# A residual turned by way of DRAM and VectorE instead of TensorE, with five smaller edits, in a two-layer hybrid kernel on one core

## The chip, the core and the metric

The kernel runs on one core of a Trainium2 chip. The core has five engines, each with its own queue of instructions, worked off in order: TensorE (PE; PEld is its weight load), VectorE (DVE), ScalarE (ACT), GpSimd (POOL) and SyncE (SP), which only issues DMAs. Engines wait for each other through semaphores. The metric is the device time of one execution in microseconds (us).

## What is computed

All in float32. Layer 0 (group norm, windowed attention, small linear layers) makes tokens `t` of shape 2 x 4096 x 128. Layer 1, which the change touches, is

```
t = t + attn(ln(t))        # full attention of 4096 tokens, 2 images
t = t + ffn(ln(t))         # STU: long convolution by FFT + three lags
```

with, cut to what matters,

```
def _L1_attn_ref(q):
    sim = einsum('blh,bmh->blm', q, q) * scale      # diagonal masked
    return einsum('blm,bmh->blh', softmax(sim), q)

def _stu(u, ...):
    return _compute_spectral(u, ...) + _compute_ar_u(Mu, u)   # spectral part + lags 0, 1, 2
```

The second line's `t` is the *residual*: the result of the attention layer, which has to be added to the ffn's result at the end. Attention leaves it with tokens on the partitions; the output needs channels on the partitions, so it has to be turned.

## The kernel before

Layer 0 fills the first 348 us and runs into the start of attention. Then, for image b = 0 and b = 1, `attention(b, fill)` walks over 36 pairs of chunks of 512 tokens. For a pair it makes scores on PE (L926, L935), exponentials on ACT (L931, L942), and two sums on PE (`other`, L1057, and `own`, L984). For most pairs the exponentials are turned by a DMA to DRAM and back (`eb`, `et`, L965) and DVE's 32 x 32 transposes (L974). The near pair (6, 7), one of the last, is turned on PE instead: `turned_here` (L976) makes four transposes of 128 x 128 on PE and one copy on DVE (L981), once at each of the pair's four steps, and the `own` product of a part comes one step after it.

After each step `fill()` lets other work run one piece further: `after(b, c)` (L1117) finishes chunk c: it divides, adds the residual in place into `tt[b]` (tokens on partitions), normalizes, turns the result and makes the forward transform; `room()` and `fresh()` (L1100, L1106) send the transform `us` to DRAM through POOL's queue, two places or so behind. `filters()` (L1338) makes the transforms of the filters into DRAM (`gs`); their negatives are written into two places in turn (L1393, L1394), each read by a store.

`short_lags(b, h)` (L1202) has two parts for each half h of an image. The first (four pieces) turns the residual: 4 x 4 PE transposes of `tt[b]` and an ACT copy of 128 x 512 into `xa[b]` (L1210). The second (four pieces) makes the lags: three matmuls of 128 x 512 in PE (L1220), and DVE adds the result, scaled, onto `xa[b]` (L1236, four or eight instructions). `residual_of` (L1399) puts the first part in the queue of fill pieces. After `attention(1)` the last chains, the remaining lags and the last residual pieces are run out (L1545 to L1561).

The ffn's main loop works in 160 *blocks*: `burst` (L1589) multiplies the loaded `ct` (filters) and `ut` (input) into four PSUM banks `pc`, which DVE and ACT copy to `y` (L1603), two banks each, and calls the loads of the block four or five further on: one `ut` and four `ct` DMAs on SP. A group of four blocks is projected (`project`, L1617, into the four banks `acc`) while the next group's bursts are put in between, one before each eight k. `mixed_bins` (L1623) combines a group: copies of `acc` on DVE and ACT (`af`), the rest on POOL. When an image's 16 groups of a chunk are there, `back` (L1648) transforms them back in eight places (par, f): PE transposes of `ob` (L1669), ACT copy `t` (L1670), and at the next step four matmuls (L1656), added by DVE onto `xa[b]` (L1662). A step is put in after k = 4 and k = 12. `finished` (L1709) and, for the last image, the tail (from L1771) add `xa` and send the output.

In the main loop only PE's order is the program's (`manual_schedule(engines={PE})`). The order on DVE, ACT, POOL and SP is laid down when the kernel is built, by a planner with its own costs. All queues are in order on the chip.

Of the kernel before, what the change touches and what calls it, by code (L numbers as in the profile page):

```python
# [14 lines left out]
P = 128  # L15
NB = 2
# [86 lines left out]
def kernel(  # L103
# [769 lines left out]

    us = dram.tile([NB, 2, Q, 2, 2, SG, FB, P], F32, name="us")
    gs = dram.tile([Q, 2, 2, SG, GROW], F32, name="gs")

    with ap_:
        tp = ap_.enter_context(tc.tile_pool(name="l1_t", bufs=1, side="right"))
# [22 lines left out]
        def attention(b, fill):  # L901
# [135 lines left out]
            for i, (a, c) in enumerate(pairs):  # L1037
# [6 lines left out]
                for j in range(4):  # L1044
                    if tt[1] is not None and not ordered:
                        ordered.append(written.enter_context(tc.manual_schedule(engines={engines.PE, engines.DVE, engines.Activation, engines.Pool, engines.SP})))
                    due = late and late[0][0] <= step
                    while following and len(coming) < min(4, j + (2 if j == 0 and a != c and not due else 1)):
                        coming.append(coming_of(*following, len(coming), coming, halves))
                    n = 4 * CHUNKS[a] + j  # L1050
                    turn = lambda v, o: v.rearrange(o, q=4, t=4) if far(a, c) else v
                    if j == 0:
                        pass_on(2)
                    if a == c:
                        onto(owns[a], n, owns[a], es[j], j == 0, a == 7 and j == 3)
                    else:
                        nc.tensor.matmul(  # L1057
                            turn(other, "p (q t j) -> p q t j"), lhsT=tok[b][:, n, :], rhs=es[j],
                            start=(j == 0), stop=(j == 3),
                        )  # L1060
                    if a != c and j == 3:
                        xs, ov = xa[b][:, chunk(c)], other
                        if far(a, c):
                            xs, ov = xs.rearrange("p (t q j) -> p q t j", t=4, q=4), ov.rearrange("p (q t j) -> p q t j", q=4, t=4)
                        if a:
                            nc.vector.tensor_tensor(xs, ov, xs, ALU.add)  # L1066
                        else:
# [49 lines left out]
        def after(b, c):  # L1117
# [84 lines left out]
        def short_lags(b, h):  # L1202


            for par in range(2):
                n0 = (par * 2 + h) * 8
                for f0 in range(0, 8, 4):
                    pt = bank()
                    transposed(pt, tt[b][:, n0 + f0 : n0 + f0 + 4, :])
                    nc.scalar.copy(xa[b][:, (n0 + f0) * P : (n0 + f0 + 4) * P], pt)  # L1210
                    yield
            for par in range(2):
                for part_ in range(2):
                    c0 = (2 * h + part_) * 512
                    py = lag_bank()
# [14 lines left out]
                    for lo, hi in cut:  # L1230
                        t0 = c0 + lo * BLK
                        s = 0 if t0 < 256 else 1 if t0 < 512 else 2 if t0 < 1024 else 3
                        for e in range(2):
                            for i in range(NFP):
                                xs = xv[:, e, i, :, p0 + lo : p0 + hi]
                                nc.vector.scalar_tensor_tensor(  # L1236
                                    xs, pv[:, e, i, :, lo:hi], seg[:, s : s + 1], xs, ALU.mult, ALU.add
                                )
                    yield

        def branch_weights():
# [95 lines left out]

        def filters():  # L1338

            negatives = cm[1][:, 3 * SG * LL : (3 * SG + 4) * LL].rearrange("p (a g c) -> p a g c", a=2, g=2)  # L1340
            ph = {}
            for (hh, e), pn in pns.items():
                at = (2 * hh + e) * LL
# [12 lines left out]

            everything = [(r0, c0 + ri * P, (ri,), P) for r0, c0 in row_tiles for ri in range(2)]
            everything.append((left_row, left_col, (0, 1), 64))
            for r0, c0, parts_, m in everything:
                places = cm[1][:, SG * LL : (3 * SG) * LL].rearrange("p (j e c) -> p j e c", j=SG, e=2)  # L1360
                for j in range(SG):
# [26 lines left out]
                            store(fb[mine], r0, n, ri, s, 1, 1)  # L1388
                    if 1 in parts_:
                        mine = slice(m - n, m)  # L1390
                        fn = negatives[:, j % 2]
# [7 lines left out]
        def residual_of(lags):  # L1399
            for _ in range(4):  # L1400
                next(lags)
                yield

        def filler(b, steps, kept, slow=()):

# [4 lines left out]
            def fill(c=None):  # L1410
                if c is not None:
                    done.append(c)
                    urgent.append(after(b, c))
                    if len(done) % 4 == 0:
                        lags = short_lags(b, len(done) // 4 - 1)
                        if kept is not None:
                            kept.append(lags)
                            lags = residual_of(lags)
                        urgent.append(lags)
                    return  # L1420

                stores()
# [119 lines left out]
        for gen in (*steps, slow):  # L1542
            for _ in gen:
                pass
        *chains, residuals = left  # L1545
        held = [step for gen in held for step in (gen,) * 4]
        held = (next(gen, None) for gen in held)
        while chains:
# [2 lines left out]
                    chains.remove(gen)  # L1551
            next(kept[0], None)
            next(held, None)
        for _ in residuals:
            next(kept[0], None)
            next(held, None)
        for _ in (*held, *kept[0]):
            pass
        lags = kept[1]
        for _ in range(2):  # L1560
            next(lags)  # L1561

# [6 lines left out]
    with ExitStack() as cv:  # L1569
# [77 lines left out]

        def back(b, chunk, places):  # L1648

            waiting = None  # L1650
            for place in (*places, None):
                if waiting:
                    par, f, t = waiting
                    py = slot().rearrange("p (a q) -> p a q", a=4)
                    for a in range(4):
                        nc.tensor.matmul(py[:, a, :], lhsT=t[:, a, :], rhs=inv[:, 4 * chunk + a, :], start=True, stop=True)  # L1656
# [6 lines left out]
                if place:  # L1663
                    par, f = place
                    t = cp.tile([P, 4, P], F32, tag="t", name="t", bufs=4)
                    pt = slot().rearrange("p (a q) -> p a q", a=4)
                    for a in range(4):
                        src = ob[:, b, chunk, a, par].rearrange("p k (o t) -> p t (k o)", t=FB)
                        nc.tensor.transpose(pt[:, a, :], src[:, FB - 1 - f], ident)  # L1669
                    nc.scalar.copy(t, pt)  # L1670
                    waiting = par, f, t
                    yield True
            yield None

# [34 lines left out]
        def finished(b):  # L1709
# [3 lines left out]
            for h in range(2):  # L1713
                o = cp.tile([P, HQ, 2, 2, FB, 2], F32, tag="o", name="o", bufs=2)
                for par in range(2):
                    for a0 in (0, 2):
# [9 lines left out]
                            send(b, h, o)  # L1726
                        yield None if h and par and a0 else True

        order_ = [(b, q) for b in range(NB) for q in range(K2)]
        to_load = order_[len(first_blocks) :]  # L1730
        ahead = list(first_blocks)
        rest = []
        with tc.manual_schedule(engines={mybir.EngineType.PE}):
            y = new_y()
            for i in range(4):
                if i % 2 == 0:
                    next(lags, None)
                burst(y, i)
            for _ in lags:
                pass  # L1740
# [7 lines left out]
            for i, (b, g) in enumerate(groups):  # L1748
# [21 lines left out]

        b = NB - 1  # L1771
        ts = [turned(b, par) for par in range(2)]
        for h in range(2):
            o = cp.tile([P, HQ, 2, 2, FB, 2], F32, tag="o", name="o", bufs=2)
            pys = [(sums(a) if h else slot()).rearrange("p (s f q) -> p s f q", s=2, f=FB) for a in range(4)]
            for a in (0, 2):
                for par in range(2):
                    nc.tensor.matmul(
                        alike(pys[a][:, par]), lhsT=ident, rhs=residual(b, par, h, a),
                        start=(par == 0), stop=False, skip_group_check=True,  # L1780
                    )
            for par in range(2):
                for f in range(FB):
                    for a in range(4):
                        last_products(pys[a][:, par], ts[par], h, f, a, bool(a % 2))
            for par in range(2):
                for a in range(4):
                    to = place_of(o, par, a)
                    if a % 2:
                        nc.vector.tensor_tensor(alike(to), alike(pys[a][:, par]), residual(b, par, h, a), ALU.add)  # L1790
                    else:
                        nc.scalar.copy(to, pys[a][:, par])
            send(b, h, o)


# [93 lines left out]
```

## Time and profile before

Three runs: median 1963.6 us (1962.83 to 1963.72). The profiled execution took 1964.29 us, of which the span from its first to its last instruction is 1962.6.

| stage | us from the start | PE busy | DVE | ACT | POOL | PE clock granted | DMA share |
|---|---|---|---|---|---|---|---|
| layer 0, then start of layer 1 | 0 to 348 | 316.9 | 284.7 | 262.0 | 223.1 | 0.97 | 0.25 |
| attention, image 0 | 348 to 747 | 392.7 | 198.2 | 120.0 | 162.1 | 1.00 | 0.64 |
| attention, image 1 | 747 to 1139 | 386.0 | 175.8 | 124.3 | 168.5 | 1.00 | 0.70 |
| last chains and lags, first bursts | 1139 to 1205 | 59.6 | 39.1 | 17.5 | 18.3 | 0.97 | 0.24 |
| ffn main loop | 1205 to 1945 | 734.8 | 251.0 | 203.4 | 165.7 | 1.00 | 0.24 |
| tail | 1945 to 1962.6 | 8.8 | 6.4 | 5.1 | 0 | 0.84 | 0.29 |

Busy times are in us. PE is busy nearly all of the time from 348 to 1945. Lines of a timeline, here and below, give the start, the duration (of a run of like instructions together), the engine, the source line and operation, what is written from what, the number, and in brackets how long the engine sat idle before it and what ended that. SPq marks an issue on SP's queue.

### The profile page before, as it was taken

Reading aid. Unit: us, or ns where it says so; the run is one execution under the profiler, and the core shown is the slowest. Engines: PE = TensorE matmul, PEld = TensorE weight load, DVE = VectorE, ACT = ScalarE, POOL = GpSimd, SP = SyncE. Lnnn points to the kernel's source line nnn. Section 1 sums busy time; section 2 is a strip of 40 time slices with the busy share of each in tenths; the row PEclk is TensorE's granted clock in tenths of the full one; section 3 lists DMA queues with packets and bytes.
Section 4 is the critical chain, followed back from the end, with each engine's and each line's share of the span. In section 5 each row is a group of like instructions: output and inputs, shape, how many; then the busy total and the mean of one; then the engine's idle time right before and its main releaser. Section 6 shows DMA issues by size and latency. Waiting matters only on the chain.

```text
span 1962.6 us, 50908 instructions
## 1 busy us (share of the span) xinstructions
PE 1898.9 (97%) x20504; PEld 1351.1 (69%) x20504; DVE 955.2 (49%) x3026; ACT 732.2 (37%) x1718; POOL 737.7 (38%) x1209
## 2 busy tenths in 40 slices
PE   6899998999999999999999998999999999999998
PEld 4677776444444444444444446999998999999987
DVE  5799997454554534354544463333333343333332
ACT  2789887323233333332333222322222222222221
POOL 4366885524643335532425331222221121222211
PEclk8999999999999999999999999999999999999999
DMA  4222221767776544877966413222222223222211
GB/s 157 61 61 60 62 61 38 158 182 215 215 204 192 151 121 123 269 209 221 252 199 185 122 53 83 66 68 66 67 68 50 59 74 87 66 68 67 66 39 44
DMA packets 249770, 226.16 MB, mean 115 GB/s; under 512 B 126815, under 2 KB 204655, under 8 KB 242112
## 3 DMA queue, kind: packets, MB, share of 16 engines
q1 hardware_dynamic: 222786, 129.15, 27.2%
q10 hardware_dynamic: 8126, 58.04, 7.6%
q0 software_dynamic: 18624, 35.72, 6.2%
q8 instruction: 163, 2.67, 0.6%
q14 instruction: 71, 0.58, 0.1%
HBM read 131.40 MB, written 91.25 MB: 113 GB/s over the span
## 4 chain that ended last, share of the span: by engine, by line
PE 79%; DVE 6%; POOL 5%; DMA 4%; issue 2%; ACT 2%; SPq 1%; DVEq 0%; POOLq 0%; ACTq 0%
PE acc L1617 29%; PE own L984 11%; PE bank L926 8%; PE other L1057 8%; PE pc L1598 7%; PE bank L349 2%; PE bank L935 2%; PE bank L202 2%; PE bank L559 1%; PE bank L1176 1%; PE bank L1220 1%; DMA et<-eb 1%; ACT p L546 1%; DMA us<-ub 1%; DMA eb<-e 1%
## 5 line engine op out<-in xcount | busy, mean ns | idle before, releaser
L1603 DVE COPY y<-pc 128x512 f32<-128x512 f32 x320 | 206.3, 686 | 346.7 <-PE pc L1598 346.4
L1617 PE MATMUL acc<-y,mpl 32*128 32x256 f32 x5120 | 323.0, 379 | 0.8 <-DVE af L1627 0.8
L1603 ACT COPY y<-pc 128x512 f32<-128x512 f32 x320 | 171.9, 589 | 393.3 <-PE pc L1598 388.7
L1617 PE MATMUL acc<-y,mmi 32*128 32x256 f32 x5120 | 315.1, 375 | 0.0
L1617 PEld LDWEIGHTS acc<-y,mpl 32*128 32x128 f32 x5120 | 289.2, 186 | 7.5 <-DVE af L1627 1.6
L1617 PEld LDWEIGHTS acc<-y,mmi 32*128 32x128 f32 x5120 | 290.7, 185 | 2.9
L1628 POOL TENSOR_TENSOR af<-af 128x512 f32<-128x512 f32 x39 | 49.7, 1275 | 578.2 <-DVE af L1627 506.1
L1057 PE MATMUL other<-e,tok 128*128 128x512 f32 x448 | 227.5, 594 | 2.3 <-DVE xa L1066 2.2
L931 ACT ACTIVATE e<-bank 128x512 f32<-128x512 f32 x216 | 129.2, 599 | 250.6 <-PE bank L926 246.3
L926 PE MATMUL bank<-cm 128*128 128x512 f32 x432 | 222.5, 601 | 0.0
L984 PE MATMUL own<-et,tok 128*128 128x512 f32 x448 | 211.9, 595 | 6.2 <-DVE et L974 3.4
L1598 PE MATMUL pc<-ct,ut 32*128 32x256 f32 x2560 | 209.3, 376 | 2.0 <-DVE y L1603 2.0
L1161 POOL TENSOR_TENSOR ub<-uo 128x256 f32<-128x256 f32 (+1 forms) x176 | 111.5, 668 | 178.8 <-ACT uo L1157 150.8
L1598 PEld LDWEIGHTS pc<-ct,ut 32*128 32x128 f32 x2560 | 170.7, 186 | 7.7 <-DVE y L1603 4.1
L974 DVE STREAM_TRANSPOSE et<-et 128x512 f32<-128x512 f32 x216 | 134.2, 679 | 75.9 <-DMA et<-eb 75.8
L984 PEld LDWEIGHTS own<-et,tok 128*128 128x128 f32 x448 | 84.5, 191 | 113.1 <-issue 91.4
L1057 PEld LDWEIGHTS other<-e,tok 128*128 128x128 f32 x448 | 81.4, 191 | 92.1 <-issue 82.4
L926 PEld LDWEIGHTS bank<-cm 128*128 128x128 f32 x432 | 76.1, 191 | 73.7 <-issue 68.1
L546 ACT ACTIVATE p<-p,mn 128x196 f32<-128x196 f32 x256 | 114.4, 449 | 14.4 <-DVE mn L536 13.7
L1092 POOL DMA_DIRECT2D us<-ub x158 | 107.8, 722 | 12.0 <-DMA us<-ub 7.4
L1157 ACT COPY uo<-bank 128x512 f32<-128x512 f32 (+1 forms) x96 | 45.5, 518 | 97.1 <-PE bank L1176 56.9
L536 DVE CUSTOM_DVE_ANT_0 p<-bank,tab 128x196 f32<-128x196 f32 x256 | 76.5, 354 | 4.9 <-PE bank L523 4.7
(267 smaller groups left out, 2591.4 us busy)
## 6 DMA issues: line engine op xcount, KB each, us to landing
eb<-e ACTq DMA_DIRECT2D x54, 1024.0 KB
et<-eb SPq DMA_DIRECT2D x216, 256.0 KB
ut<-us SPq DMA_DIRECT2D x156, 128.0 KB
us<-ub POOLq DMA_DIRECT2D x54, 256.0 KB, 5.0
vw<-vd SPq DMA_DIRECT2D x256, 49.0 KB
ct<-gs SPq DMA_DIRECT2D x312, 40.0 KB
ct<-gs SPq DMA_DIRECT2D x312, 32.0 KB
vd<-v SPq DMA_DIRECT2D x128, 32.0 KB
```

The source lines that it names most:

```text
L536: nc.vector.tensor_tensor_reduce(t[name + "p"][:, h, :], t[name + "S"][h][:, 0:KEYS], tab[:, ci, h, :], 1.0, 3.0e38, ALU.add, ALU.min, t[n ...
L546: nc.scalar.activation(p, p, AF.Exp, bias=t[name + "mn"][:, h : h + 1], scale=-1.0, accum_out=t["den"][:, u, h : h + 1],)
L926: nc.tensor.matmul(ps.rearrange("p (q t j) -> p q t j", q=4, t=4), lhsT=cm[b][:, n * P : (n + 1) * P], rhs=keys.rearrange("p (t q j) -> p ...
L931: nc.scalar.activation(e, ps.rearrange("p (q t j) -> p q t j", q=4, t=4), AF.Exp, bias=0.0, scale=ASCALE)
L974: in_place(nc.vector.transpose(part, part))
L984: nc.tensor.matmul(out_, lhsT=tok[b][:, n, :], rhs=e, start=first, stop=last, skip_group_check=True)
L1057: nc.tensor.matmul(turn(other, "p (q t j) -> p q t j"), lhsT=tok[b][:, n, :], rhs=es[j], start=(j == 0), stop=(j == 3),)
L1092: by.dma_start(out=to, in_=part)
L1161: adder[sgn].tensor_tensor(ub[:, sgn, 0:n], both[:, 0:n], both[:, n : 2 * n], op)
L1598: nc.tensor.matmul(pcs[j].rearrange("p (g o c) -> p o g c", g=4, o=2)[:, :, at], lhsT=ut[rows_, par, :], rhs=cv_[rows_], start=True, stop= ...
L1603: (nc.scalar.copy if j % 2 else nc.vector.tensor_copy)(y[:, :, :, 4 * kl + j, :], pcs[j].rearrange("p (g x k) -> p k g x", g=4, k=KF))
L1617: nc.tensor.matmul(acc[j][:, 0:256], lhsT=(mmi if l else mpl)[rows_, k, :], rhs=y[rows_, k, 2 * l : 2 * l + 2].rearrange("p s n x -> p (s ...
```

## The change

Six edits:

1. *Residual.* The PE transposes and ACT copies of `short_lags` go, and `residual_of` with them. `after` sends `kept_`, 128 x 512 of `tt[b]`, to a DRAM tensor `rd` as soon as it is done (16 stores of 256 KB, by `fresh`). In the ffn a new generator `residuals` loads each of the 16 chunks back with 16 DMAs on SP (32 partitions x 4 runs of 32 floats each), turns it in place with one DVE transpose of 128 x 512, and adds it onto `xa[b]` with one POOL instruction. Its tile `rt` has one buffer. The program calls one step at every burst of the main loop: four loads a step, and a fifth step for transpose and add.
2. *Lags.* They are written to `xa[b]` and not added; half of the instructions go to ACT. All four pieces of the last half are put between the first four bursts; before, two were, and two came ahead.
3. *Negatives* have eight places, in `tok[1]`, which is free then.
4. *Near pair (6, 7).* Its four turned parts are made in its first two steps, two in each.
5. *back* does two places a step, and steps are put in after k = 4 only.
6. *Tail.* Products of 128 columns for each parity come first, then all evictions; before, products of 64 columns for each half of the channels' columns, and that half's evictions.

```diff
+    rd = dram.tile([NB, NT // 4, P, 4, P], F32, name="rd")
...
-                        turned_here(here, es, j)
-                        late.append((step + 1, a, c, here, j))
+                        for m in (2 * j, 2 * j + 1) if j < 2 else ():
+                            turned_here(here, es, m)
+                            late.append((step + 1, a, c, here, m))
...
             nc.vector.tensor_tensor(kept_[:, :, P - 1], kept_[:, :, P - 1], rest, ALU.subtract)
+            fresh(rd[b, c], kept_)
...
-            for par in range(2):
-                n0 = (par * 2 + h) * 8
-                for f0 in range(0, 8, 4):
-                    pt = bank()
-                    transposed(pt, tt[b][:, n0 + f0 : n0 + f0 + 4, :])
-                    nc.scalar.copy(xa[b][:, (n0 + f0) * P : (n0 + f0 + 4) * P], pt)
-                    yield
...
-                                nc.vector.scalar_tensor_tensor(
-                                    xs, pv[:, e, i, :, lo:hi], seg[:, s : s + 1], xs, ALU.mult, ALU.add
-                                )
+                                if i:
+                                    nc.scalar.activation(
+                                        xs, pv[:, e, i, :, lo:hi], AF.Identity, bias=0.0, scale=seg[:, s : s + 1]
+                                    )
+                                else:
+                                    nc.vector.tensor_scalar(xs, pv[:, e, i, :, lo:hi], seg[:, s : s + 1], None, ALU.mult)
...
-            negatives = cm[1][:, 3 * SG * LL : (3 * SG + 4) * LL].rearrange("p (a g c) -> p a g c", a=2, g=2)
+            negatives = tok[1].rearrange("p n c -> p (n c)").rearrange("p (a g c) -> p a g c", g=2, c=LL)
...
-            for place in (*places, None):
-                if waiting:
-                    par, f, t = waiting
+            for now_ in (*(places[i : i + 2] for i in range(0, len(places), 2)), []):
+                for par, f, t in waiting:
...
+        def residuals():
+            for b in range(NB):
+                for c in range(NT // 4):
+                    rt = cp.tile([P, 4, 4, 32], F32, tag="rt", name="rt", bufs=1)
+                    for j in range(4):
+                        for q in range(4):
+                            nc.sync.dma_start(
+                                out=rt[32 * q : 32 * q + 32, :, j],
+                                in_=rd[b, c].rearrange("(h p) j (q i) -> q j p h i", h=4, q=4)[q, j],
+                            )
+                        yield
+                    flat = rt.rearrange("p h j i -> p (h j i)")
+                    nc.vector.transpose(flat, flat)
+                    xs = xa[b][:, c * 512 : (c + 1) * 512].rearrange("p (j h r) -> p h j r", j=4, h=4)
+                    nc.gpsimd.tensor_tensor(xs, rt, xs, ALU.add)
+                    yield
...
             for i in range(4):
-                if i % 2 == 0:
-                    next(lags, None)
+                next(lags, None)
                 burst(y, i)
...
                             burst(following, 2 * l + k // 8)
+                            next(to_add, None)
                         project(y, acc, l, k)
-                        if rest and k in (4, 12):
+                        if rest and k == 4:
```

*The built order.* On PE, the changed kernel differs from the one before by these edits alone. On the queues that the planner fills, the new instructions stand as follows. SP, in the ffn: after the load set (one `ut`, four `ct`) of block n come the rt loads

```
block n   rt loads behind its set (chunk: number)
4         0: 8
5         0: 7
6         0: 1
7         1: 3
8         1: 13, 2: 11
9         2: 5,  3: 16
10        4: 16, 5: 9
11        5: 7,  6: 16
12        7: 16, 8: 8
13        8: 8,  9: 16
14        10: 16, 11: 8
15        11: 8, 12: 16
16        13: 16, 14: 8
17        14: 8, 15: 16
18 on     none
```

The first load of a chunk waits for POOL (the add of the chunk before), and nearly every DMA of the queue waits for the one eight places ahead of it. On DVE the 16 transposes stand between the copies `y` of blocks 3 to 15: one behind the first copy of block 3, one or two behind those of each block from 4 to 14. On POOL six adds stand ahead of the first group's `mixed_bins`, six ahead of the second's, four ahead of the third's.

More of the change, by code (lines that the diff above doesn't have):

```diff
@@ L1358, in filters @@
             everything.append((left_row, left_col, (0, 1), 64))
+            taken = 0
             for r0, c0, parts_, m in everything:
@@ L1390, in filters @@
                         mine = slice(m - n, m)
-                        fn = negatives[:, j % 2]
+                        fn = negatives[:, taken % negatives.shape[1]]
+                        taken += 1
                         one, two = sums[mine, 0, :], sums[mine, 1, :]
@@ L1397, in filters @@
                     yield True
[L1399 to L1402, printed above, removed]
         def filler(b, steps, kept, slow=()):
@@ L1414, in fill @@
                     if len(done) % 4 == 0:
[L1415 to L1419, printed above, removed]
+                        kept.append(short_lags(b, len(done) // 4 - 1))
                     return
@@ L1544 @@
                 pass
-        *chains, residuals = left
+        chains = list(left)
         held = [step for gen in held for step in (gen,) * 4]
@@ L1553 @@
             next(held, None)
-        for _ in residuals:
-            next(kept[0], None)
-            next(held, None)
         for _ in (*held, *kept[0]):
@@ L1559 @@
         lags = kept[1]
-        for _ in range(2):
-            next(lags)
     outf = out.rearrange("b c h w -> b c (h w)")
@@ L1648, in back @@
         def back(b, chunk, places):
-            waiting = None
-            for place in (*places, None):
-                if waiting:
-                    par, f, t = waiting
+            waiting = []
+            for now_ in (*(places[i : i + 2] for i in range(0, len(places), 2)), []):
+                for par, f, t in waiting:
                     py = slot().rearrange("p (a q) -> p a q", a=4)
@@ L1662, in back @@
                         nc.vector.tensor_tensor(xv[:, e], pv, xv[:, e], ALU.add)
-                if place:
-                    par, f = place
+                waiting = []
+                for par, f in now_:
                     t = cp.tile([P, 4, P], F32, tag="t", name="t", bufs=4)
@@ L1670, in back @@
                     nc.scalar.copy(t, pt)
-                    waiting = par, f, t
+                    waiting.append((par, f, t))
+                if now_:
                     yield True
@@ L1727, in finished @@
                         yield None if h and par and a0 else True
+        def residuals():
[14 more added lines that the diff above has]
+                    yield
+        to_add = residuals()
         order_ = [(b, q) for b in range(NB) for q in range(K2)]
@@ L1772 @@
         ts = [turned(b, par) for par in range(2)]
+        pys = [[sums(a) if par else slot() for a in range(4)] for par in range(2)]
+        half = [[[py.rearrange("p (f h c) -> p h f c", f=FB, h=2)[:, h] for h in range(2)] for py in of] for of in pys]
+        for a in (0, 2):
+            for par in range(2):
+                for h in range(2):
+                    nc.tensor.matmul(
+                        alike(half[par][a][h]), lhsT=ident, rhs=residual(b, par, h, a),
+                        start=(h == 0), stop=False, skip_group_check=True,
+                    )
+        for par in range(2):
+            for f in range(FB):
+                for a in range(4):
+                    rows_ = slice(32 * a, 32 * a + 32)
+                    nc.tensor.matmul(
+                        pys[par][a][:, f * CQ : (f + 1) * CQ], lhsT=ts[par][rows_, f, :],
+                        rhs=inv[rows_, K2 // BC * 4, :], start=bool(a % 2), stop=True, skip_group_check=True,
+                    )
         for h in range(2):
             o = cp.tile([P, HQ, 2, 2, FB, 2], F32, tag="o", name="o", bufs=2)
[L1775 to L1785, printed above, removed]
             for par in range(2):
@@ L1789 @@
                     if a % 2:
-                        nc.vector.tensor_tensor(alike(to), alike(pys[a][:, par]), residual(b, par, h, a), ALU.add)
+                        nc.vector.tensor_tensor(alike(to), alike(half[par][a][h]), residual(b, par, h, a), ALU.add)
                     else:
-                        nc.scalar.copy(to, pys[a][:, par])
+                        nc.scalar.copy(to, half[par][a][h])
             send(b, h, o)
```

## The prediction

> **What bounds the kernel now.** First the engines' busy shares and the chain of waits on the page.
>
> ```profile
> PE 1898.9 (97%) x20504; PEld 1351.1 (69%) x20504; DVE 955.2 (49%) x3026; ACT 732.2 (37%) x1718; POOL 737.7 (38%) x1209
> ...
> PE 79%; DVE 6%; POOL 5%; DMA 4%; issue 2%; ACT 2%; SPq 1%; DVEq 0%; POOLq 0%; ACTq 0%
> ```
>
> TensorE (PE) is busy 97% of the span and carries 79% of the chain. In both attentions and in the ffn it is almost never idle, so PE work taken out there is time gained, and whatever makes PE wait there is time lost. Second, the ffn's steady state: the timeline of SP's queue (start, duration, operation).
>
> ```profile
> 1305.21 0.37 SPq L1494 DMA_DIRECT2D ut<-us  x1
> 1305.62 2.45 SPq L1486 DMA_DIRECT2D ct<-gs  x4
> ```
>
> Every 4.32 us (one burst of products, 0.86, and eight projections, 3.45) SP issues five loads in 2.8 us and is free for 1.5 us. A queue that looks idle is two thirds full. Third, what one issue costs, in the views of single lines (minimum, median, maximum in ns):
>
> ```profile
> L965 SPq DMA_DIRECT2D et<-eb x216: 302/431/2957, 368.8 to 1100.5; - x108
> ...
> L1486 SPq DMA_DIRECT2D ct<-gs x624: 512/602/1996, 1048.0 to 1901.8; - x156
> ...
> DMA to landing us min/median/max: 1.9/3.6/6.3
> ```
>
> The last line is ct's time from issue to landing.
>
> **What the change takes from PE.** (1) *Transposes.* short_lags turned 64 blocks on PE, in 16 groups of four. Groups follow the next work at 0.43 us:
>
> ```profile
> 683.12 0.60 PE L202 MATMUL bank<-ident,tt 128*128 128x128 f32 x4
> 683.56 1.02 PE L926 MATMUL bank<-cm 128*128 128x512 f32 x2
> ```
>
> 683.56 - 683.12 = 0.44. Twelve groups lie inside the attentions: 12 x 0.43 = **-5.2**. The other four are in (3). The ACT copies (L1210, 586 ns) were beside PE.
>
> (2) *Two places a step for the pair (6, 7).*
>
> ```profile
> PE own L984 <- DVE et L981: 2.8, 2, 1.4
> ```
>
> PE waited 1.4 us at the end of each attention for the last turned part. Now all four parts are turned in the first two steps, so the copies are early: **-2.8**. Next late there is DVE's own list, which is no longer: bounds -2.8 to 0.
>
> (3) *From attention to ffn.* PE rows before:
>
> ```profile
> 1176.49 0.66 PE L202 MATMUL bank<-ident,tt 128*128 128x128 f32 x4
> ...
> 1181.43 0.65 PE L202 MATMUL bank<-ident,tt 128*128 128x128 f32 x4 [2.02 <-ACT uo L1157]
> 1181.92 7.11 PE L1220 MATMUL bank<-tt,mu 128*128 128x512 f32 x12
> 1190.34 2.81 PE L1220 MATMUL acc<-tt,mu 128*128 128x512 f32 x6 [1.31 <-DVE xa L1236]
> ```
>
> The residual's transposes wait for banks that ACT's uo copies free (last at 1184.5, held by us stores), then twelve matmuls take 7.1 us where six take 2.6, then the first sum waits for DVE. The first projection starts at 1205.0. In the new order PE reaches its first sum into acc 4.0 us earlier (1.4 from (2), 2.6 from a lag that moves into attention 0, a move and no gain), at 1172.5, and waits for the last uo copy, at about 1180.5; then come four lags and four bursts, 4 x (2.58 + 0.86) = 13.8, and a burst with its wait, 1.8: projections start at 1196.1, 8.9 earlier, of which 1.4 is counted and 2.6 is moved: **-4.9**. Lags written (not added), half on ACT, only shorten evictions. The two rd stores now ahead of the us stores on SP are 2 x 0.5 us long before these; bounds -8 to 0.
>
> (4) *Negatives.* Eight places instead of two end DVE's wait for earlier gs stores (8.4 us of DVE), but PE idled only 2.4 us between 400 and 560: **-0.5**, bounds -2.4 to 0.
>
> (5) *back, two places a step.*
>
> ```profile
> 1492.16 1.16 PE L1656 MATMUL pc<-inv,t 128*128 128x128 f32 x8
> 1493.16 0.64 PE L1669 MATMUL pc<-ident,ob 128*128 128x128 f32 x4
> 1493.73 1.58 PE L1617 MATMUL acc<-y,mpl 32*128 32x256 f32 x24
> 1495.13 1.04 PE L1598 MATMUL pc<-ct,ut 32*128 32x256 f32 x16
> 1495.99 2.34 PE L1617 MATMUL acc<-y,mmi 32*128 32x256 f32 x40
> 1498.26 1.16 PE L1656 MATMUL pc<-inv,t 128*128 128x128 f32 x8
> ```
>
> A period with a step is 6.10 against 4.32: 1.78 more, while its matmuls need 0.86 + 0.44 = 1.30. An interruption costs 0.48. Nine steps become five, for two images: 8 x 0.48 = **-3.9**. A step now takes four pc buffers of four; its evictions (two DVE pairs of 0.76, two ACT copies of 0.58) end within 1 us, and the next burst comes after 1.5 us of projections, so nothing waits. finished keeps its nine steps, further apart: 0.
>
> (6) *Tail.* 64-wide products
>
> ```profile
> 1951.07 2.01 PE L1698 MATMUL pc<-inv,t 32*128 32x64 f32 x64
> ...
> 1952.91 1.97 PE L1698 MATMUL acc<-inv,t 32*128 32x64 f32 x64
> 1953.15 1.94 DVE L1790 TENSOR_TENSOR o<-pc,xa 128x256 f32<-128x256 f32 x4 [5.16 <-PE pc L1698]
> ```
>
> become half as many of 128. At 29 ns a record (1.88 / 64) the first parity is done after 32 records, 0.95 us, where the first half took 1.9; eight DVE evictions then run on without a gap: **-0.9**.
>
> Sum: -5.2 - 2.8 - 4.9 - 0.5 - 3.9 - 0.9 = **-18.2**.
>
> **What the change adds.** Sixteen rd stores: 14 on POOL at 0.70 (L1092), 9.8 us, where POOL is idle over half of the time: 0. In the ffn: 256 rt loads, 16 DVE transposes at 0.67 (L974, same shape), 16 POOL adds at 1.28 (L1628). Averaged over twenty groups they would fit. But only PE's order is fixed by the program. In the built order, which the section on the change lists, SP issues all 256 loads between the load sets of blocks 4 to 18, up to 25 in one gap; and DVE has all 16 transposes before burst 15's copies. rt has one buffer, so chunk c+1's first load waits for POOL's add of chunk c. Queued behind the waiting load on SP are ut and ct of the coming bursts; behind the waiting transpose on DVE are the y copies that free PE's pc banks. PE waits for both.
>
> No row shows an rt load (32 partitions x 4 runs of 128 bytes). By the nearest, et<-eb (also 32 x 4 runs), an issue is 0.43; ends 0.30 (its minimum) and 0.73 (vw<-vd, L510). Landing: 3.0 taken, between ct's minimum and median since an rt load has half of its bytes; ends 1.9 and 3.6. One chunk: 16 x 0.43 = 6.9, landing after the last issue 2.6, transpose 0.67, add 1.28, hand-overs 0.2: 11.6. Sixteen: 186. Of the 14 ut/ct sets in between (0.37 + 4 x 0.60 = 2.8) eight fall inside a chunk: 22. With the first load 6.2 after the first lag of the ffn, burst 16 starts at 6.2 + 208 = 214.5 or so. At its own pace: 13.8 + 0.9 + 12 x 4.32 = 66.5. **+148.** At the ends a chunk is 8.5 or 16.6: +99 or +228. After the last chunk the old pace returns.
>
> **Two rules of the Trainium skill.** "DMA: Bandwidth & Descriptors", section on the anatomy of one DMA, puts a DMA at about 2.0 us fixed plus its bytes, with some 50 ns at the sequencer. The rows say 366 to 725 ns on SP, back to back. By the rule, with eight loads in flight (each waits for the one eight before it), a chunk is two rounds of 2.04 plus 2.1 = 6.2: +61 instead of +148. The row decides. "TensorE: Matmul & The Clock Gate", part 1, has the clock halve after an idle window of some 3.4 us: this speaks against the change, which makes PE idle for 10 us at a time. The profile grants 0.84 in the half-idle last 17.6 us and 1.00 in the ffn. At half clock twelve periods would take 52 us more of PE; PE is not on that chain, so 0 is taken.
>
> **The sum.** Own time 1964.3 - 18.2 + 148 = 2094; the median of the runs lies 0.7 below it: **2093**.
>
> **Rivals.** (A) The forecast, 2044 to 2173 with its ends: 0.78. (B) The chain is there but issues are cheap, as by the rule: 1964.3 - 18.2 + 61 - 0.7 = 2006. For it: lanes and latency, not SP, may set the pace. Against: the five loads every 4.32 us occupy SP for 2.8. 0.12. (C) *Faster*: the loads flow beside the bursts and nobody waits, 1964.3 - 18.2 - 0.7 = 1945. It holds from a chunk of (66.5 - 6.2 - 22) / 16 = 2.4 us downward. For it: 1.5 us of SP free per period, DVE a third busy; spaced as the text has them (16 loads in five periods) they'd need 6.9 + 13.9 of 21.6 us. Against: the built order, and one landing alone is 1.9 at least. 0.05. (D) Landing at ct's maximum, 6.3, and PE at half clock on the path: chunk 14.9, +200 + 52: 2197. 0.05.
>
> **Numbers.** The range reaches below A's lower end and to A's upper end: 2035 to 2180. What a run can tell from no change is about 0.2%, 4 us. Faster is C: 0.05; same 0.01 (a gain and a small chain that cancel); slower 0.94.
>
> **What would show it.** Right: after about 1196 a stretch of some 200 us with PE busy two to four tenths, its wait on DVE's y copies; rt transposes waiting for DMA in sum over 100 us; SP issuing rt loads at 0.4 to 0.6 without pause. (1): no tt transposes, attention 1 ending 6 to 8 us earlier. (5): five steps some 11.7 us apart (two bare periods and 3.1). (6): last evictions start about 1 us after the first product. Wrong: PE busy over 90% right after the first projection, or chunks closer than 5 us.

## The result, and the profile after

The changed kernel takes 2104.5 us (median of five runs, 2099.97 to 2107.08) against 1962.8 us of the kernel before on the same chip: 1.0721 times as long, interval 1.0704 to 1.0737. The prediction was 2093, range 2035 to 2180. The profiled execution took 2099.97 us, its span is 2098.3, 135.7 more than the span of before.

First the same two rows of the page, busy shares and the chain of waits by engine.

```profile
PE 1919.2 (91%) x20376; PEld 1370.1 (65%) x20376; DVE 958.6 (46%) x3002; ACT 735.4 (35%) x1742; POOL 765.9 (36%) x1239
...
PE 76%; SPq 7%; DVE 5%; POOL 5%; DMA 4%; issue 2%; ACT 1%; ACTq 0%; DVEq 0%; POOLq 0%
```

TensorE executes 128 instructions fewer and yet is busy for 20 us more: part of its work ran at a lower clock. SP's queue, 1% of the chain before, is 7% now. Where that lies is seen in the busy time by stretch (length, busy time of PE, PEld, DVE, ACT and POOL with their counts, granted clock, DMA share, GB/s). I cut at the same events in both kernels: end of layer 0, end of the attentions, first sum of a lag into acc, burst 16. The changed kernel from the first sum of a lag to burst 16, and from there to the end:

```profile
1171.80:1392.70 220.90, 103.34 (x1050) 86.26 (x1050) 34.24 (x61) 22.57 (x46) 28.47 (x37) 0.70 0.21 41
1392.70:2098.30 705.60, 689.50 (x12192) 671.67 (x12192) 240.96 (x431) 193.01 (x390) 157.88 (x371) 0.99 0.24 64
```

And before, the first of these two:

```profile
1190.30:1256.05 65.75, 63.75 (x1034) 57.55 (x1038) 24.30 (x44) 18.48 (x36) 8.50 (x20) 1.00 0.28 71
```

The second lasted 706.55 us before. So +155.2 us lie between the first lag of the ffn and burst 16, -0.9 behind it, and -18.5 ahead of it (-2.9 of these in layer 0, which the change does not touch: it ended at 345.3 to 351.2 us in the profiles of this case). In the long stretch PE is under half busy, at a granted clock of 0.70. Its waits there, by who ended them (line waited at, engine and line that released it: us in total, times, longest):

```profile
PE pc L1585 <- DVE y L1590: 94.2, 11, 16.2
PE acc L1604 <- DVE af L1614: 22.7, 2, 11.4
```

Both are copies on DVE that free banks. And what DVE waited for, in the same stretch:

```profile
DVE rt L1729 <- DMA rt<-rd: 162.8, 15, 13.6
```

DVE had nothing to do for 163 us but wait, with the transpose of rt at the head of its queue and the copies behind it. One chunk, first in the timeline of SP's queue (start, duration, operation):

```profile
1238.88 2.46 SPq L1478 DMA_DIRECT2D ct<-gs  x4
1241.97 15.03 SPq L1723 DMA_DIRECT2D rt<-rd  x25
```

Then in DVE's timeline (in brackets the idle time before it and what ended it):

```profile
1239.89 0.71 DVE L1729 STREAM_TRANSPOSE rt<-rt 128x512 f32<-128x512 f32 x1 [10.21 <-DMA rt<-rd]
1250.82 0.71 DVE L1729 STREAM_TRANSPOSE rt<-rt 128x512 f32<-128x512 f32 x1 [10.21 <-DMA rt<-rd]
1251.45 1.25 DVE L1590 COPY y<-pc 128x512 f32<-128x512 f32 x2
```

And in GpSimd's:

```profile
1240.69 1.26 POOL L1731 TENSOR_TENSOR xa<-rt,xa 128x512 f32<-128x512 f32 x1 [10.83 <-DMA ct<-gs]
```

And in PE's:

```profile
1252.16 2.67 PE L1585 MATMUL pc<-ct,ut 32*128 32x256 f32 x16 [15.51 <-DVE y L1590]
```

(The bracket in GpSimd's row names a ct load; the transpose that the add needs ended at 1240.60, 0.09 us before the add.) The transpose at 1239.89 is added by GpSimd until 1241.95; SP issues the next chunk's first load at 1241.97, the sixteenth some 7 us later, and at 1250.82 the next transpose runs: a chunk of 10.93 us. The two y copies that burst 8 had been waiting for run only then, at 1251.45, and burst 8 starts at 1252.16.

### The profile page after: what moved, and what is told of

Read it like the earlier page. It is cut to its first block, busy times and chain, and to the rows that moved or that the text cites. A ratio compares the mean times of both kernels' runs of the same rounds, so it can differ in the third digit from the quotient of the medians.

```text
span 2098.3 us, 51106 instructions
## 1 busy us (share of the span) xinstructions
PE 1919.2 (91%) x20376; PEld 1370.1 (65%) x20376; DVE 958.6 (46%) x3002; ACT 735.4 (35%) x1742; POOL 765.9 (36%) x1239
## 4 chain that ended last, share of the span: by engine, by line
PE 76%; SPq 7%; DVE 5%; POOL 5%; DMA 4%; issue 2%; ACT 1%; ACTq 0%; DVEq 0%; POOLq 0%
PE acc L1604 25%; PE own L985 11%; PE bank L927 8%; PE other L1058 8%; PE pc L1585 6%; SPq L1723 5%; PE bank L349 2%; PE bank L936 2%; PE bank L559 2%; PE bank L1179 1%; PE bank L202 1%; DMA et<-eb 1%; PE bank L523 1%; POOL xa L1731 1%; DMA rt<-rd 1%
## 5 line engine op out<-in xcount | busy, mean ns | idle before, releaser
L1604 PE MATMUL acc<-y,mpl 32*128 32x256 f32 x5120 | 331.0, 387 | 23.4 <-DVE af L1614 23.4
L1604 PE MATMUL acc<-y,mmi 32*128 32x256 f32 x5120 | 323.9, 383 | 0.0
L1604 PEld LDWEIGHTS acc<-y,mpl 32*128 32x128 f32 x5120 | 299.1, 191 | 31.8 <-DVE af L1614 26.2
L1585 PE MATMUL pc<-ct,ut 32*128 32x256 f32 x2560 | 223.3, 393 | 94.9 <-DVE y L1590 94.2
L1604 PEld LDWEIGHTS acc<-y,mmi 32*128 32x128 f32 x5120 | 302.0, 191 | 2.8
L1585 PEld LDWEIGHTS pc<-ct,ut 32*128 32x128 f32 x2560 | 178.8, 193 | 105.9 <-DVE y L1590 98.6
L1731 POOL TENSOR_TENSOR xa<-rt,xa 128x512 f32<-128x512 f32 x16 | 20.2, 1263 | 192.1 <-DVE rt L1729 120.4
L1729 DVE STREAM_TRANSPOSE rt<-rt 128x512 f32<-128x512 f32 x16 | 11.4, 711 | 172.6 <-DMA rt<-rd 162.8
```

The costliest lines, as they stand in the source:

```text
L1585: nc.tensor.matmul(pcs[j].rearrange("p (g o c) -> p o g c", g=4, o=2)[:, :, at], lhsT=ut[rows_, par, :], rhs=cv_[rows_], start=True, stop= ...
L1604: nc.tensor.matmul(acc[j][:, 0:256], lhsT=(mmi if l else mpl)[rows_, k, :], rhs=y[rows_, k, 2 * l : 2 * l + 2].rearrange("p s n x -> p (s ...
```

## The experiments

Differences are taken against the kernel before on the same chip, since chips differ: its median was 1962.8 us beside the changed kernel, 1968.5 beside experiments 1, 2, 6 and 7, 1965.3 beside the others. "Stall" below is the difference to the kernel without the reload, which stands at -15.2 us: 141.7 + 15.2 = 157 us for the changed kernel. It compares kernels across chips, so a few us of it may be the chips'. In the cuts of code, "..." stands for lines left out, and `mybir.EngineType.` is left out before the engines' names.

**1. Without the reload.**

```
-        to_add = residuals()
+        to_add = iter(())
```

> The changed kernel without the reload: the turned residual is still stored to DRAM, but it is neither loaded, turned nor added, so the output lacks the attention's residual. Theory: what is left is the gain of the other parts. The trace of the changed kernel puts it at 18.5 us up to the first sum into acc and about 5 in the two-place steps, less 1 or so in the tail: 1942. By the sum of the prediction 1945. If a part of the stall came from something else (the lags, the two-place steps), it stays above 1955.

1953.3 us, ratio 0.9921 (0.9907 to 0.9936), -15.2 us; its output lacks the residual. The whole loss belongs to the reload, and the other parts bring a gain that is smaller than the 18.2 of the prediction and the 21 that I expected here.

**2. Every engine in the order of the text.**

```
-        with tc.manual_schedule(engines={PE}):
+        with tc.manual_schedule(engines={PE, DVE, Activation, Pool, SP}):
```

> The changed kernel with every engine of the ffn's loop, SP among them, held to the order of the text: four rt loads after each burst, in 64 of the 80 bursts, the transposes one burst behind. Theory (the place of the loads in SP's queue made the stall): the stall of about 150 us goes, and the time is that of the kernel without the reload, near 1945, at most 1955. Rival (the 256 issues cost SP what they take, wherever they stand): a burst's five loads plus four rt loads take SP 2.9 + 1.7 = 4.6 us against a period of 4.32, so 64 x 0.3 = 18 us are left: 1963. Rival (DVE's transposes or GpSimd's adds stop the y copies by themselves): 16 x 2 or more, 1977.

2017.4 us, ratio 1.0239 (1.0219 to 1.0259), +48.9 us: 93 of the 157 us of stall are gone, 64 are left. All three numbers of the expectation missed. SP's timeline, five load sets and one chunk:

```profile
1232.29 1.81 SPq L1723 DMA_DIRECT2D rt<-rd  x4
1234.44 2.71 SPq L1478 DMA_DIRECT2D ct<-gs  x4
1237.25 0.53 SPq L1486 DMA_DIRECT2D ut<-us  x1
1237.83 2.90 SPq L1723 DMA_DIRECT2D rt<-rd  x4
1240.78 2.46 SPq L1478 DMA_DIRECT2D ct<-gs  x4
...
1249.97 1.89 SPq L1723 DMA_DIRECT2D rt<-rd  x4
...
1259.13 1.84 SPq L1723 DMA_DIRECT2D rt<-rd  x4
```

From 1232.29 to 1259.13 there is hardly a gap: 26.8 us for what has to fit into five periods of 4.32, 21.6 us. The transposes still held DVE (78.3 us of waits for rt between 1205 and 1510), but SP itself waited only 5.7 us in that stretch, so its issues set the pace. So the rival with SP's occupation has the mechanism, but I had made it too cheap: without pauses four rt issues span up to 2.9 us instead of 1.7, and an ut issue 0.53 instead of 0.37.

**3. VectorE, ScalarE and GpSimd in the order of the text, SP left to the planner** (the line above without SP).

> The changed kernel with VectorE, ScalarE and GpSimd held to the order of the text in the ffn's loop, SP left to the planner, which now puts each chunk's sixteen loads in one run, every fifth burst. SP per five bursts: 5 x 2.9 + 16 x 0.43 = 21.4 us by the median issue, 22.8 by the 0.52 that the two-buffer kernel showed back to back, of 21.6. Expected: 0 to 20 over the kernel without the reload, so -15 to +5 against before. If loads and issues cost as much as in the program-paced kernel (26.7 us for five sets and their sixteen loads): +49.

2000.6 us, ratio 1.0179 (1.0161 to 1.0197), +35.3: a stall of 50 us, where 0 to 20 were expected. The loads now come in runs of sixteen:

```profile
1248.83 8.94 SPq L1723 DMA_DIRECT2D rt<-rd  x16
1257.87 0.38 SPq L1486 DMA_DIRECT2D ut<-us  x1
...
1274.64 8.67 SPq L1723 DMA_DIRECT2D rt<-rd  x16
1283.40 0.38 SPq L1486 DMA_DIRECT2D ut<-us  x1
```

One cycle is 1283.40 - 1257.87 = 25.5 us, again for what has to fit into 21.6: sixteen rt issues take 8.7 to 8.9 us and not 6.9, five load sets 16.8 and not 14.5. PE's largest wait in the ffn is now for ut itself (25.3 us in nine waits), not for DVE. So with DVE's queue in order, what is left of the stall is SP's time, bunched or spread.

**4. The loads on GpSimd's queue, in the planner's order.**

```
-                            nc.sync.dma_start(
+                            nc.gpsimd.dma_start(
                                 out=rt[32 * q : 32 * q + 32, :, j],
```

> The changed kernel with its loads on GpSimd's queue instead of SP's, in the planner's order: SP is left to the loads of ct and ut, but DVE still has all sixteen transposes between the y copies of the first fourteen blocks or so. If SP's queue alone made the stall (ct and ut late), it goes: -15 to -5 against before. If the transposes in DVE's queue stop the y copies by themselves: a chunk is 16 x 0.7 + 2.6 + 0.7 + 1.3 + 0.2 = 16 us, sixteen 256, against some 67 at the own pace: +190 over the kernel without the reload, +175 against before.

2111.2 us, ratio 1.0746 (1.0726 to 1.0767), +145.9: the full stall, though SP issues no rt load. PE's longest wait over the run:

```profile
PE pc L1585 <- DVE y L1590: 97.3, 11, 20.0
```

DVE's, between 1180 and 1420:

```profile
DVE rt L1729 <- DMA rt<-rd: 174.5, 16, 14.0
```

And that of SP's queue, in the same stretch:

```profile
SPq L1486 <- PE pc L1585: 176.8, 17, 26.0
```

SP now waits 177 us for PE: ct and ut could have come any time. The transposes in DVE's queue stop the kernel by themselves, each for as long as its chunk's loads take to be issued and land. The size was below the 175 expected mainly because GpSimd's issue took 0.55, not 0.70. ScalarE and GpSimd are in the planner's order here too; that it is DVE's queue is read from the waits, not tested apart.

**5. The loads on GpSimd's queue, every engine in the order of the text** (experiments 2 and 4 together).

> The program-paced kernel with all sixteen loads a chunk, of 128-byte runs, but issued by GpSimd instead of SP. Theory (SP's occupation is what kept 64 us of the stall in the paced kernel): SP is back at 2.9 us of 4.32, and the stall goes: -15 to -5 against before; GpSimd has 4 x 0.7 = 2.8 us more to issue in four of five periods, and would be some 88% occupied, so its bins could come a little late. Rival (the small runs, the DMA engines or the waits set it): as with SP, +45 to +50.

1952.6 us, ratio 0.9935 (0.9922 to 0.9949), -12.7. The stall is 2.4 us, which is within what the runs scatter. Same 256 loads, same bytes; only the queue of the loads and the order on the engines in the ffn's loop differ from the changed kernel. GpSimd between 1300 and 1400:

```profile
1300.00:1400.00 100.00, 100.00 (x1856) 99.83 (x1852) 37.55 (x64) 28.65 (x59) 69.76 (x136) 1.00 0.35 79
```

Here its issues count as busy: 70 of 100 us, and PE has no gap.

**6. Two buffers**, a single one of sd making room.

```
-            sd = cp.tile([P, 2, 128], F32, tag="sd", name="sd", bufs=2)
+            sd = cp.tile([P, 2, 128], F32, tag="sd", name="sd", bufs=1)
...
-                    rt = cp.tile([P, 4, 4, 32], F32, tag="rt", name="rt", bufs=1)
+                    rt = cp.tile([P, 4, 4, 32], F32, tag="rt", name="rt", bufs=2)
```

> The changed kernel with two rt buffers (and one sd buffer in place of two, to make room; GpSimd writes and reads sd in turn). The order of loads stays as bunched as before. Theory: the wait for landing, transpose and add (about 4 us of each 10.9 us chunk) is hidden and SP's own issues are left: 256 x 0.43 + 12 load sets x 2.9 = 145 us from the first load to the last, against 208 measured; the time falls by about 63, to 2040. If the single buffer is the whole cause: about 1950. If landing or the DMA engines set the pace: no change, 2100.

2073.3 us, ratio 1.0529 (1.0513 to 1.0545), +104.8, a stall of 120: 37 us less, not 63. The wait for the add is gone, and the issues follow each other at 0.52 us (thirty in 15.58), so SP needs 162 us from the first load to the last where I had 145.

**7. Four loads a chunk**: rd is laid out by quarters, stored by four stores and read by four loads.

```
-    rd = dram.tile([NB, NT // 4, P, 4, P], F32, name="rd")
+    rd = dram.tile([NB, NT // 4, 4, P, 4, 32], F32, name="rd")
...
-            fresh(rd[b, c], kept_)
+            for q in range(4):
+                fresh(rd[b, c, q], kept_[:, :, 32 * q : 32 * q + 32])
...
-                    for j in range(4):
-                        for q in range(4):
-                            nc.sync.dma_start(
-                                out=rt[32 * q : 32 * q + 32, :, j],
-                                in_=rd[b, c].rearrange("(h p) j (q i) -> q j p h i", h=4, q=4)[q, j],
-                            )
+                    for q in range(4):
+                        nc.sync.dma_start(
+                            out=rt[32 * q : 32 * q + 32],
+                            in_=rd[b, c, q].rearrange("(h p) j i -> p h j i", h=4),
+                        )
```

> The changed kernel with the residual laid out in DRAM by quarters, stored by four stores a chunk instead of one, and loaded by four loads a chunk (32 partitions x 4 runs of 512 bytes) instead of sixteen; the same bytes, and again an order that the planner bunches. Theory (issues plus one chain of landing, transpose and add per chunk): a chunk takes 4 x 0.45 + 2.6 + 0.7 + 1.3 + 0.2 = 6.6 us, 16 of them 106 and some six load sets inside 17, against about 54 at the own pace from the same point: +74 over the kernel without the reload, 2016, and up to 10 more for 48 more stores in the attentions. Rival (only the issues count, the chain is hidden): a quarter of the stall, 1980. Rival (bytes or landing set the pace): about 2090.

2018.6 us, ratio 1.0253 (1.0237 to 1.0268), +50.1. The chain of the first theory, a stall of 65: with few issues it is landing, transpose and add, one chunk after another, that hold DVE.

**8. Four loads a chunk and the order of the text.**

> Both former edits together: four loads a chunk, and the ffn's loop in the order of the text, so one rt load follows each burst in 64 of 80 bursts. Theory (SP's occupation per period decides: 2.9 + 0.5 = 3.4 us of 4.32): the stall is gone, and the time is that of the kernel without the reload, 15 us below before, less 0 to 5 for 48 more stores in the attentions: -15 to -10 against before. If the wait for landing, transpose or add has a cost of its own even when spaced: 16 x 2 to 4 us more, +20 to +50.

1954.2 us, ratio 0.9946 (0.9931 to 0.9962), -11.2: the stall is 4 us. So the wait for a chunk has no price of its own once nothing stands behind it.

**9. The same, and the last evictions in the order of the text.**

```
+        with tc.manual_schedule(engines={DVE, Activation, SP}):
+            for h in range(2):
+                o = cp.tile([P, HQ, 2, 2, FB, 2], F32, tag="o", name="o", bufs=2)
...
```

> As the one before, and the last evictions in the order of the text, so that the first half of the output is complete after eight evictions of the sixteen and is sent while the others run. Theory: in the changed kernel both halves were complete 0.4 us apart, 3.3 us after the first eviction, and their two transfers ended together; sent apart as before the change, the tail is 1.2 us shorter. Otherwise no difference.

1953.3 us, ratio 0.9944 (0.9929 to 0.9959), -12.1; the times don't tell it from number 8, the traces do. From the first of the last products (L1792) to the end of the span it takes 11.0 us against 12.3 in number 8.

**10. The kernel before with only the near pair, the places of negatives and the two-place steps.**

> The kernel before, with only the near pair's two places a step, the other places for negatives, and the two places a step in back: the residual stays on TensorE and the lags are added as before. Expected by the prediction's terms -2.8 - 0.5 - 3.9 = -7.2 us against before; by the changed kernel's trace, where the steps of back gave 5.2, -8.5. If back's gain needs the rest of the change: -3.

1952.2 us, ratio 0.9940 (0.9917 to 0.9963), -13.2; its span is 11.0 us shorter than that of before. That is more than the -7.2 and -8.5 expected, though the interval reaches from -16 to -7. Three small edits that leave the residual on TensorE bring as much as the best of the versions above; what moving the residual adds to them, once it stalls nothing, is not to be told from zero here.

**11. Loads on GpSimd's queue, order of the text, the last evictions too** (experiments 5 and 9 together).

> The program-paced kernel with the loads on GpSimd's queue, and the last evictions in the order of the text: the two former gains together, -13 and 1 us of the tail: -14 against before.

1950.0 us, ratio 0.9929 (0.9915 to 0.9944): -15.3 by the medians, the fastest version of the full computation that was run, though its interval overlaps those of 5, 8, 9 and 10.

## Why the prediction was right, point by point

**The stall** was forecast at 148 us. From the first sum into acc to burst 16 the changed kernel took 220.9 us, the kernel without the reload 1174.9 to 1247.6, 72.7: a difference of **148.2**. (By the medians of all runs, across chips, it is 157.) The mechanism is shown by experiments 4 and 5, but the exact hit is in part luck. Both stretches were some 6 us longer than forecast (220.9 against 214.5, 72.7 against 66.5), which the difference hides; for the second, step (3) says why. A chunk without a load set inside it took 10.93, not 11.6: its sixteen issues 7.42 (6.9 forecast), from there to the transpose 1.43 (2.6 forecast), then 2.08 for transpose, add and hand-overs. So a load landed about 1.9 us after its issue and not 3.0, as where GpSimd issues it (experiment 4; minimum, median, maximum):

```profile
DMA to landing us min/median/max: 1.8/1.9/3.9
```

Against that, the load sets inside the chunks cost more than my 22: from the first add to the last it is 194.4 us, less 15 x 10.93, leaves 30. Two errors of some 10 us cancelled.

I had named two queues, SP's and DVE's, and given the price to SP's issues. Both count, but not equally: with no rt load on SP the planner's order still makes the whole stall, by DVE's waits (experiment 4); SP's issues, with the other engines in the order of the text, make 50 to 64 us of it (experiments 2 and 3). SP's part in the changed kernel is mainly that it sets how long a chunk takes.

**Rivals.** B, cheap issues, is out: it needs chunks of 6.2 us, and none took less than 10.8. The 50 ns of the Trainium skill's page "DMA: Bandwidth & Descriptors" (section on the anatomy of one DMA) are given there for a DMA that GpSimd issues, as one part of its cost; an rt load took 0.55 us of GpSimd's queue (experiment 4) and 0.43 of SP's. C had a wrong term: spaced as the text has them, the loads were to need 6.9 + 13.9 of 21.6 us of SP. They took 26.8, so pacing alone would not have made the change faster. D's slower clock was there, granted 0.70 in the stall, but the twelve periods hid behind the chunks as I had argued.

**(1) Transposes, (2) near pair, (4) negatives**, -8.5 together. From the end of layer 0 to the end of the attentions: 790.9 before, 785.4 after, with two lags (2 x 2.58) inside that stood behind it before: **-10.7**. The sum is near, its terms are not. Experiment 10, which keeps the transposes and has the same lags inside, took 788.5: (2) and (4) alone gave -7.6 where I had -3.3, and (1) is left with -3.1 where I had -5.2. For (2), the wait for et at L981 (2.8) is gone as forecast. In the stretch from 400 to 560, where I had looked for the effect of (4), a wait of 2.2 us for an xa sum of DVE (L1066) is gone too; I had taken 0.5 from the bounds -2.4 to 0, and the low end fits. The rest was not taken apart. For (1), I had put the sixteen rd stores at 0. But all eleven kernels that have them show, early in the second image, a wait of 3.1 to 4.6 us for an et load that neither before nor experiment 10 has. In the changed kernel:

```profile
776.98 3.65 PE L985 MATMUL own<-et,tok 128*128 128x512 f32 x4 [3.17 <-DVE et L975]
```

Eight kernels, the changed one and those of experiments 1 to 6 and 11, run the same instructions in the attentions. They took 785.4 to 791.8 us for the stretch (one trace each), five of them more than the 788.5 of experiment 10. So the changed kernel's trace is the best of the eight, and in most of them waits took the saved 5.2 us of PE work back. Whether the stores make these waits, or other transfers that moved with them, was not tested.

**(3) Transition**, -4.9: **this step failed**, by the restart of the clock and by what a lag and a burst cost. Up to the first sum into acc it is close: 51.2 us before, 41.1 after, less 5.2 of moved lags, -4.9, where the times of the forecast make -5.8. PE waits 8.0 us for the last uo copy, as forecast. But what follows took longer. In the kernel without the reload (wait, then the restart in two rows):

```profile
1166.70:1174.90 8.20, 0.06 (x4) 0.01 (x1) 1.85 (x5) 1.92 (x4) 3.75 (x5) 0.70 0.40 127
1174.90:1181.40 6.50, 6.50 (x23) 2.59 (x23) 0.76 (x3) 0.37 (x1) 0.56 (x1) 0.59 0.23 71
1181.40:1190.00 8.60, 8.52 (x48) 4.28 (x44) 3.82 (x9) 3.51 (x8) 0.00 (x0) 1.00 0.26 67
```

A lag and a burst at the clock of the third row, and the lag behind them:

```profile
1186.17 2.84 PE L1216 MATMUL acc<-tt,mu 128*128 128x512 f32 x6
1188.94 1.15 PE L1585 MATMUL pc<-ct,ut 32*128 32x256 f32 x16
1190.02 2.84 PE L1216 MATMUL acc<-tt,mu 128*128 128x512 f32 x6
```

In the second row PE has no gap, and a lag and a burst take 6.5 us at a granted 0.59. At 1.00 they take 3.85 (1186.17 to 1190.02); I had reckoned with 3.44. From the first sum to the first projection it is 21.5 us, before it was 14.7; I had 15.6. Of these 5.9 us too much, the slow clock makes 2.6 (6.5 less 3.85), the size of four pairs 1.6 (4 x 0.41), and waits for y copies probably the rest. So the step gave -4.9 + 6.8 = **+1.9**. I had weighed the Trainium skill's page "TensorE: Matmul & The Clock Gate" (part 1: half rate after an idle window of some 3.4 us) at the stall, where it costs nothing, and not at the 8 us wait that I had worked out myself, where it stands on the path. The rows of before held a sign of it: the twelve matmuls that took 7.11 us, where two groups of six take 5.2, followed waits of 0.35 to 2.02 us, and from 1182 to 1190.3 the granted clock was 0.80.

**(5) back**, -3.9. A step in the changed kernel:

```profile
1634.38 2.34 PE L1604 MATMUL acc<-y,mmi 32*128 32x256 f32 x40
1636.65 2.05 PE L1642 MATMUL pc<-inv,t 128*128 128x128 f32 x16
1638.54 1.12 PE L1655 MATMUL pc<-ident,ob 128*128 128x128 f32 x8
1639.59 1.58 PE L1604 MATMUL acc<-y,mmi 32*128 32x256 f32 x24
1640.99 1.04 PE L1585 MATMUL pc<-ct,ut 32*128 32x256 f32 x16
```

Two places cost 3.15 us here (a period of 7.47 less 4.32), where one cost 1.78. Over the periods that hold steps, the time above bare periods was 17.8 and 19.4 us for the two images before and 16.0 and 16.0 after: **-5.2**. finished took 0.5 more.

**(6) Tail**, -0.9. PE at the end, in its timeline:

```profile
2086.43 1.17 PE L1792 MATMUL pc<-inv,t 32*128 32x128 f32 x32
2087.43 1.07 PE L1792 MATMUL acc<-inv,t 32*128 32x128 f32 x32
```

DVE's timeline:

```profile
2087.66 1.93 DVE L1802 TENSOR_TENSOR o<-pc,xa 128x256 f32<-128x256 f32 x4 [4.32 <-PE pc L1792]
2089.44 1.89 DVE L1802 TENSOR_TENSOR o<-acc,xa 128x256 f32<-128x256 f32 x4
```

SP's queue, after and before:

```profile
2090.96 0.83 SPq L1694 DMA_DIRECT2D out_dram<-o  x2
1955.15 2.10 SPq L1707 DMA_DIRECT2D out_dram<-o  x2
```

The evictions do start 0.84 us earlier, counted from the first of the last products. But they go by pc and acc, that is by parity, and each half of the output needs both parities: the two transfers are issued within 0.83 us, at the end, where before the two issues spanned 2.10 us and the first transfer ran beside the last evictions. From the first eviction to the end it is 10.6 us instead of 9.4. In sum **+0.3**. What I had left out is the transfer behind the evictions; experiment 9, which sends the halves apart again, is 1.3 shorter here than number 8.

The terms as measured are -10.7 + 1.9 - 5.2 + 0.5 + 0.3 = -13.2; the kernel without the reload was 12.1 shorter by its span and 15.2 by the medians, against my 18.2. Behind burst 16 the changed kernel itself shows only -0.9: its first 7.3 us there still ran at a granted clock of 0.61, while the kernel without the reload is 3.7 shorter in that stretch.

## What to carry to other kernels

Work that is meant to fill idle time of an engine is safe only if, in the order that is built, nothing urgent stands behind it: read the in-order queues, and ask of each new waiting instruction what is next in line, before adding up free time. An idle DMA system says nothing of the queue that issues into it; count issues times their measured duration against the period, with room to spare, and prefer few large loads or another queue. And where a change makes TensorE wait on its path, add the slow restart to the wait. And transfers put at nothing because their queue has room may make others late: compare the waits of the stage where they run.

## What the runs showed of the hardware

- One rt load took 0.43 us of SP's queue by the median in the changed kernel and in experiments 2, 3 and 6. Over a run of sixteen the mean was 0.46 (7.42 us, changed kernel) to 0.56 (8.94 us, experiment 3), because single issues were longer (minimum, median, maximum in ns; first the changed kernel, then experiment 3):

```profile
L1723 SPq DMA_DIRECT2D rt<-rd x16: 309/430/432, 1242.0 to 1249.0; - x16
L1723 SPq DMA_DIRECT2D rt<-rd x16: 430/430/1467, 1248.8 to 1257.3; - x16
```

  An ut load took 0.37 us with pauses and 0.53 to 0.54 without. What makes the difference was not separated; each load also waits for the one eight before it, which these runs left in place.
- The same rt loads took 0.55 us each from GpSimd's queue, evenly (0.548 to 0.619), and landed 1.9 us (experiment 4) or 2.2 us (experiments 5 and 11) after, by the median.
- After a wait of 8 us TensorE ran the next 6 us at a granted clock of 0.59 to 0.62, and in the kernel without the reload at 1.00 from there; in the stall, with idle stretches of 5 to 16 us, it was 0.70 on average. After the waits of 3.0 to 4.6 us for et in the attentions, the next four matmuls took 2.0 to 3.8 us; after those of 0.3 to 1.4 us, 2.0 us by the traces of before and of experiments 6, 9 and 10.
